# A memory set between gathers, gates turned at two places, and reciprocals spread later, in a two-layer mixture-of-experts kernel

## The chip, the cores and the metric

One core of a Trainium2 chip. The metric is the device time of one execution in microseconds, as the median of several runs. Times inside an execution come from a profiled execution, counted from the start of its span.

## What is computed

Two transformer layers over x of 8 batches x 256 tokens x 128 channels, all in float32. Each layer is modulated: six rows per batch (`sa, ca, ga, sb, cb, gb`) are made from a small matrix product.

```python
h = layernorm(x) * (1 + ca) + sa
x = x + ga * attention(h)                # causal, 16 heads
h = layernorm(x) * (1 + cb) + sb
x = x + gb * ffn(h)
```

Layer 0's heads have 8 channels, layer 1's 64. Layer 0's ffn is a shared expert (128 to 512 to 128, gelu) plus 8 routed experts of the same shape, of which each token takes the best two by softmax, weighted by their normalised shares. Layer 1's ffn returns `h + shared(h) + sum of two of 16 experts`, each `silu(h wg) * (h wu) @ wd` with 64 hidden channels, chosen by sigmoid scores.

## The kernel before

The kernel is written in a tile framework on bass. The order of instructions on every engine is the order of the program text; the framework inserts the waits between engines from the reads and writes of tiles. A tile with a tag takes one of the tag's `bufs` buffers and waits for the last readers of what was in it. A general path at the end runs only if a number called `bad` says so.

Tokens are in 16 tiles of 128, four to a group `w` (0 to 3), two to a batch `b`. Layer 0's attention is a loop of 24 units (three a batch), layer 1's of 32 (four a batch). Work that is not attention (norms, routing, moving tokens) is hung on units through three tables: `at(n, ...)` runs early in unit n, `at_end(n, ...)` at its end, in the order of registration, `at_head(n, head, ...)` behind the mask of a head.

**Routing.** A token is sent to its experts by an indirect DMA that GpSimd issues (a scatter, L932), into a DRAM table `xs` sorted by expert. Tiles of 128 rows of `xs` then go through their expert, results are written to the DRAM table `ys` (by SP), and indirect DMAs bring them back by token (a gather, L1058). `Sorted.gather(yg, j)` issues two for token tile j. In layer 0, each scatter follows a memory set of one column on GpSimd, `apart_on_gpsimd` (L1404): `nc.gpsimd.memset(most, P - 0.5)`. The tile `most` (L1076) is also a constant of the program: `flag` (L2023) compares a count of good softmax sums with it to make `bad`. `flag` comes in two steps: a reduction on VectorE (`whole`, L2026), then a matmul `good_cnt` and, on VectorE, the comparison L2030:

```python
cnt = pp.tile([1, 1], F32, tag="s", name="good_cnt")
nc.tensor.matmul(out=cnt, lhsT=whole, rhs=nums[:, 1:2], start=True, stop=True)
nc.vector.tensor_scalar(bad, cnt, most[0:1, :], 1.0, ALU.is_lt, ALU.mult)
```

**Layer 0's gates.** After routing, each token's weights stand in `gates`; `turn_gates0(w)` (L1283) transposes four tiles' gates on PE into a PSUM tile `gp` of the tag "p" (two buffers, shared with norms, logits, ranks, and projections) and copies them to SBUF as `gT`, which later multiplies the experts' output biases (L1306). `first_gates` makes the first eight tiles' gates at the end of units 17 and 20. For w = 0 and 1 the turning stands at the end of unit 23, the last; for w = 2 and 3 it stands inside the loop over layer 0's expert tiles.

**Layer 1's end.** After the last attention unit, the last batch's softmax sums are inverted (`reciprocals1`, L1708). `spread_last(us)` (L1727) spreads them over partitions: for each of two head groups u, two matmuls `rp` (L1733) into a PSUM tile of the tag "s" (two buffers), and a product into `ou` on VectorE (L1737); `finish1` (L1739) reads it. Interleaved with it, groups of four expert tiles pass through `turn1(m)` (transposes `xT` on PE, a copy on ScalarE, the next row load on SP), `hidden1(m)` (matmuls `gu` into tag "s", Silu on ScalarE, product `aq` on VectorE) and `project_tiles(m)` (matmuls `yq` into one buffer each of the tags "o" and "sum", two copies on VectorE, the write to `ys`). `norms[0]` and `norms[1]` are the norms of the last two batches in steps, `go6` and `go7` their routing steps, `tables` VectorE work that makes the tables of rows.

Then come, in the text: `gather1(j)` for the twelve token tiles of groups 0 to 2 (24 gathers); `gate_rows` and shared-expert work; `flag`'s first step; and group 3, which goes through all its experts densely. `dense_hidden(p)` is four matmuls `gud` into a buffer of tag "s", a Silu on ScalarE (L1936) and a product on VectorE (L1937), which frees the buffer. `flag`'s second step stands between `dense_hidden(2)` and `dense_hidden(3)`. `dense_gate`, `dense_project`, `combine1` (matmuls that add the gathered rows, L2018), and `ffn1_add` follow to the end.

Of the kernel before, what the change touches and what calls it, by code (L numbers as in the profile page):

```python
# [557 lines left out]
def fast_path(ctx: ExitStack, tc: tile.TileContext, i: dict, out: bass.AP, bad: bass.AP):  # L558
# [3 lines left out]
    nc = tc.nc  # L562
# [15 lines left out]
    def ps_ln(shape, name):  # L578
        return pp.tile(shape, F32, tag="p", name=name)
# [281 lines left out]
    class Sorted:  # L861
# [190 lines left out]
                in_offset=bass.IndirectOffsetOnAxis(ap=self.widx[:, d : d + 1], axis=0),  # L1052
            )

        def gather(self, yg, j):

            for k in range(2):
                nc.gpsimd.indirect_dma_start(  # L1058
                    out=yg[:, k, :], out_offset=None, in_=self.ys[:, :],
                    in_offset=bass.IndirectOffsetOnAxis(ap=self.yidx[:, j, k : k + 1], axis=0),  # L1060
                )
# [13 lines left out]
    SPANS0 = ((0, 2), (2, 2), (4, 1), (5, 1), (6, 1), (7, 1))  # L1075
# [126 lines left out]
    def norm0(bs):  # L1202

        kept = []
        name = f"0b{bs[0]}"

        def tokens():
            b, half = bs[0] // 2 * 2, bs[0] % 2
            if not half:
                tokens0["all", b] = ap0.tile([P, 4, P], F32, tag="ht", bufs=2, name=f"ht{name}")  # L1210
            ht = tokens0[bs] = tokens0["all", b][:, bass.ds(2 * half, 2 * bs[1]), :]
            if bs[1] == 1:
                tp = ps_ln([P, 2, P], f"tp{name}")
                for j in range(2):
                    nc.tensor.transpose(tp[:, j, :], h[b // 2][:, bass.ts(2 * half + j, P)], ident)
                nc.scalar.copy(ht, tp)
                return
            nc.gpsimd.tensor_tensor(by_batch(ht), by_batch(kept[0]), rows_of_span(mdb0[:, CB - 1], bs), ALU.mult)
            nc.gpsimd.tensor_tensor(by_batch(ht), by_batch(ht), rows_of_span(mdb0[:, SB - 1], bs), ALU.add)

        first = 2 * (bs[0] % 2)
        return [
            *layernorm_parts(
                bs[0] // 2, md[0], SB, CB, name, ps_ln, lambda w, xn: kept.append(xn),
                range(first, first + 2 * bs[1]),
            ),
            tokens,
        ]
# [54 lines left out]
    def turn_gates0(w):  # L1283
        gp = ps_ln([P, P], f"gp0_{w}")
        nc.tensor.transpose(gp, gates[:, bass.ts(w, TT), :].rearrange("p j e -> p (j e)"), ident)
        gT = hid0["g", w] = ap0.tile([P, P], F32, tag="gT", bufs=2, name=f"gT0_{w}")
        if w < 2:
            nc.scalar.copy(gT, gp)
        else:
            nc.vector.tensor_copy(gT, gp)  # L1290

    def shared_project0(w):
        for _ in shared_project_steps0(w):
# [100 lines left out]
    def at_end(n, *steps):  # L1394
        ends.setdefault(n, []).extend(steps)
# [28 lines left out]
    for w in range(1, NW):  # L1424
        measure, normalise, modulate = layernorm_parts(w, md[0], SA, CA, f"0a{w}", ps_ln)
        n = 6 * w - 6
# [6 lines left out]
    ways = {}  # L1433
# [9 lines left out]
    for bs in SPANS0[:4]:  # L1443
        n = 3 * sum(bs) + 2
# [18 lines left out]
    at_end(17, first_gates)  # L1463
    at_end(20, first_gates)
    norm6, norm7 = norm0(SPANS0[4]), norm0(SPANS0[5])
    at_end(23, norm6[0], lambda: turn_gates0(0), lambda: turn_gates0(1), lambda: ways[SPANS0[3]]())

    project0(0)
    project_v0(0)
# [7 lines left out]
    z1 = Sorted(xp, "1", E1, 3 * TT, ND1)  # L1477
# [93 lines left out]
    for _ in range(4):  # L1571
        hides[2]()
    one(shared_add0(1))()
    turn0(0)
    later = {
        1: tables, 2: tables, 3: tables, 5: lambda: turn_gates0(2), 7: lambda: turn_gates0(3),
        6: lambda: judge(rs0.rearrange("p b s k m -> p (b s k m)")),
    }
# [148 lines left out]
    def spread_last(us):  # L1727

        aT = st1["ou", B - 1]
        for u in us:  # L1730
            rp = pp.tile([P, 2, S], F32, tag="s", name=f"rp1_{u}")
            for m in range(2):
                nc.tensor.matmul(  # L1733
                    out=rp[:, m, :], lhsT=sel[:, u, m].rearrange("p n d -> p (n d)"), rhs=st1["r", B - 1],
                    start=True, stop=True,
                )
            nc.vector.tensor_tensor(aT[:, :, u, :], aT[:, :, u, :], rp, ALU.mult)  # L1737
# [118 lines left out]
    def weights1(m, t):  # L1856

        rows = bass.ts(t % 2, I1)
        if m < E1 // 4:
            e = 4 * m + t  # L1860
            return w1["wg1"][:, bass.ts(e, I1)], w1["wu1"][:, bass.ts(e, I1)], w1["wd1"][rows, e // 2, :]
        wt = sq["w", m]
        return wt[:, t, 0:I1], wt[:, t, I1 : 2 * I1], wt[rows, t, 2 * I1 :]

    def turn1(m):
        xT_ps = ps_ln([P, 4, P], f"xT1_{m}")
        xg = sq.pop(("x", m))
        for t in range(4):
            nc.tensor.transpose(xT_ps[:, t, :], xg[:, t, :], ident)
        xT = sq["xT", m] = lp.tile([P, 4, P], F32, tag="xT", name=f"xTs1_{m}")  # L1870
        nc.scalar.copy(xT, xT_ps)
        if m + 4 < NQ:
            fetch_rows1(m + 4)

    def hidden1(m):
        xT = sq.pop(("xT", m))
        gu = pp.tile([P, 2, 2, P], F32, tag="s", name=f"gu1_{m}")
        for what in range(2):
            for t in range(4):
                nc.tensor.matmul(  # L1880
                    out=gu[bass.ts(t % 2, I1), what, t // 2, :], lhsT=weights1(m, t)[what],
                    rhs=xT[:, t, :], start=True, stop=True,
                )
        a = sq["a", m] = lp.tile([P, 2, P], F32, tag="aq", name=f"aq1_{m}")
        nc.scalar.activation(a, gu[:, 0], AF.Silu)
        nc.vector.tensor_tensor(a, a, gu[:, 1], ALU.mult)

    def project_tiles(m):
        a = sq.pop(("a", m))
        y = [pp.tile([P, 2, P], F32, tag=tag, bufs=1, name=f"yq1_{m}_{tag}") for tag in ("o", "sum")]  # L1890
        for t in range(4):
            k = t % 2
            nc.tensor.matmul(
                out=y[k][:, t // 2, :], lhsT=a[bass.ts(k, I1), t // 2, :], rhs=weights1(m, t)[2],
                start=True, stop=True,
            )
        ysb = lp.tile([P, 2, 2, P], F32, tag="ysb", bufs=3, name=f"ysb1_{m}")
        for k in range(2):
            nc.vector.tensor_copy(ysb[:, :, k, :], y[k])
        nc.sync.dma_start(  # L1900
            out=z1.ys[bass.ds(4 * m * P, 4 * P), :].rearrange("(t p) c -> p t c", p=P),
            in_=ysb.rearrange("p a k c -> p (a k) c"),
        )
# [93 lines left out]
    sums, diags = {}, {}  # L1997

    def gather1(j):
        k, n = divmod(j, 3)  # L2000
        if n == 0:
            sums["yg", k] = lp.tile([P, 3, 2, P], F32, tag="pt", bufs=4, name=f"yg1_{k}")
        z1.gather(sums["yg", k][:, n], j)

    def weigh1(w):

# [36 lines left out]
    for j in range(2):  # L2043
        gather(1, j)
# [8 lines left out]
    for j in range(2):  # L2053
        at_head(0, 1 + 2 * j, lambda j=j: gather(2, j))
        at_head(1, 1 + 2 * j, lambda j=j: gather(3, j))
    at_end(1, lambda: combine(2))
    at_end(2, lambda: combine(3))
    for w in range(1, NW):
        n = 8 * w
# [10 lines left out]
    for b in range(B - 1):  # L2070
        n = 4 * b + 6 if b < B - 2 else N - 1
        at(n, *[lambda b=b, u=u: normalise1(b, u) for u in range(4)])
        at_end(n, lambda b=b: finish1(b))
    for bs in ((0, 2), (2, 2), (4, 1), (5, 1)):
        n = 4 * sum(bs) + 2
# [66 lines left out]
    norms[0][0]()  # L2142
    project_tiles(2)
    hidden1(4)
    spread_last((0, 1))
    turn1(5)
    norms[0][1]()
    project_tiles(3)
    norms[0][2]()
    spread_last((2, 3))  # L2150
    turn1(6)
    project_tiles(4)
    hidden1(5)
    go6()
    finish1(B - 1)
# [25 lines left out]
    for j in range(TT * LAST):  # L2181
        gather1(j)
# [54 lines left out]
def adaln_two_layers(tc: tile.TileContext, i: dict, out: bass.AP):  # L2237
    nc = tc.nc
    with tc.tile_pool(name="flag", bufs=1) as fp:
        bad = fp.tile([1, 1], mybir.dt.int32, name="bad")  # L2240
        fast_path(tc, i, out, bad)
        redo = nc.values_load(bad[0:1, 0:1], min_val=0, max_val=1, skip_runtime_bounds_check_because="a comparison")
        with tc.If(redo > 0):
            general_path(tc, i, out)
# [84 lines left out]
```

## Time and profile before

| | |
|---|---|
| median of 3 runs | 571.47 us (570.83 to 574.68) |
| profiled execution | 605.66 us, its span 603.8 us |
| mean granted TensorE clock in it | 0.963 |
| busy in the span | PE 541.5 us (90%), DVE 322.0 (53%), POOL 271.1 (45%), ACT 263.4 (44%) |

Engines are PE (TensorE), DVE (VectorE), ACT (ScalarE), POOL (GpSimd) and SP (which issues the ordinary DMAs). The page gives the span in 40 equal slices of 15.1 us, with the busy share of each engine in tenths. A line of the timeline has start, duration, engine, line of the kernel, operation, output and inputs, shapes, and in brackets the idle time before it and what ended it. A line of the waits has who waited, for what, and the sum, the number and the longest of the waits in us. PE's ends are modelled; an idle engine that nothing waits for costs nothing.

### The profile page before, as it was taken

What the parts mean: (1) busy time and instruction counts of PE and PEld (TensorE: products, weight loads), DVE (VectorE), ACT (ScalarE), POOL (GpSimd) and SP (SyncE); (2) the same over time, 40 slices, a digit from 0 to 9 for tenths busy, and PEclk for the clock granted to TensorE, in tenths of its full rate; (3) what the DMA queues carried; (4) which work ended last, traced back from release to release, by engine and by line L of the source; (5) the groups of instructions that cost most, each with busy time, mean ns of one, the idle gap of its engine ahead of it and who ended that gap; (6) DMA issues with size and microseconds to landing.
All of it is one profiled execution on the core that took longest, in us unless ns stands there. A gap on an engine that the chain in (4) does not pass through costs nothing.

```text
span 603.8 us, 11998 instructions
## 1 busy us (share of the span) xinstructions
PE 541.5 (90%) x4499; PEld 384.0 (64%) x4499; DVE 322.0 (53%) x986; ACT 263.4 (44%) x494; POOL 271.1 (45%) x400
## 2 busy tenths in 40 slices
PE   5999988899999998999999999999989988980594
PEld 4355544467999996666766676767657666840164
DVE  5258784675422224564466657556483867660153
ACT  3678765344566632664344433462535332250110
POOL 5224575665444213756222645331563540687300
PEclk9999997899999999999999999999999999986698
DMA  8699994134999812203030221203030365662311
GB/s 279 242 400 406 393 358 181 62 104 129 313 338 350 288 34 100 94 23 89 10 72 7 53 54 48 56 3 71 18 89 10 86 181 166 174 144 55 82 39 56
DMA packets 53566, 85.40 MB, mean 141 GB/s; under 512 B 6652, under 2 KB 32764, under 8 KB 52348
## 3 DMA queue, kind: packets, MB, share of 16 engines
q1 hardware_dynamic: 45308, 60.50, 31.6%
q0 software_dynamic: 8048, 23.67, 12.3%
q8 instruction: 37, 0.61, 0.4%
q10 hardware_dynamic: 144, 0.39, 0.2%
q14 instruction: 29, 0.24, 0.1%
HBM read 53.46 MB, written 31.07 MB: 140 GB/s over the span
## 4 chain that ended last, share of the span: by engine, by line
PE 72%; DVE 13%; issue 6%; DMA 3%; ACT 3%; SPq 1%; POOL 1%; another core or an unknown queue 0%; DVEq 0%; POOLq 0%; ACTq 0%
PE sc L1670 6%; PE hp L1353 6%; PE yt L1361 6%; PE o L1692 6%; PE qp L1639 5%; PE sc L1120 5%; PE y L1745 4%; PE kp L1639 4%; PE vp L1652 4%; PE o L1154 3%; PE sum L1700 3%; PE gud L1942 3%; PE hp L1273 2%; PE qk L1084 2%; PE ysh L1302 1%
## 5 line engine op out<-in xcount | busy, mean ns | idle before, releaser
L822 POOL TENSOR_SCALAR_AFFINE_SELECT pt<-pt 128x256 f32<-128x256 f32 (+1 forms) x144 | 68.0, 499 | 154.6 <-ACT pt L1673 115.3
L1058 POOL DMA_INDIRECT yg<-ys,yidx x56 | 54.4, 971 | 38.8 <-DMA ys<-ysb 20.4
L1673 ACT ACTIVATE pt<-sc 128x768 f32<-128x768 f32 x64 | 48.4, 808 | 26.2 <-PE sc L1670 26.1
L1136 ACT ACTIVATE pt<-sc 128x1024 f32<-128x1024 f32 x48 | 46.6, 1027 | 21.6 <-PE sc L1120 15.8
L1670 PEld LDWEIGHTS sc<-q,k 64*128 64x128 f32 x512 | 41.5, 187 | 18.9 <-issue 13.9
L1670 PE MATMUL sc<-q,k 64*128 64x256 f32 (+1 forms) x512 | 50.5, 336 | 0.0
L1692 PE MATMUL o<-pt,v 128*64 128x256 f32 (+1 forms) x512 | 49.0, 332 | 1.7 <-DVE ou L1704 1.7
L1355 ACT ACTIVATE hst<-hp,wt 128x128 f32<-128x128 f32 x136 | 38.9, 369 | 25.7 <-ACT hst L1355 24.6
L1655 ACT COPY v<-vp 128x512 f32<-128x512 f32 x32 | 18.8, 587 | 67.1 <-PE vp L1652 67.1
L1050 POOL DMA_INDIRECT wt<-in_wpk_dram,widx x31 | 29.6, 953 | 33.8 <-PE xT L1344 28.8
L1692 PEld LDWEIGHTS o<-pt,v 128*64 128x64 f32 x512 | 32.0, 136 | 18.9 <-POOL pt L822 5.7
L1643 DVE COPY q<-qp 128x512 f32<-128x512 f32 x32 | 22.0, 689 | 36.4 <-PE qp L1639 36.4
L1120 PE MATMUL sc<-qm,k 32*128 32x512 f32 x192 | 36.0, 726 | 3.8 <-ACT pt L1136 3.2
L1639 PE MATMUL qp<-h,wq 128*128 128x256 f32 x128 | 36.0, 404 | 3.3 <-DVE q L1643 2.0
L1366 DVE COPY ysb<-yt 128x128 f32<-128x128 f32 x39 | 11.4, 292 | 50.0 <-PE yt L1361 50.0
L932 POOL DMA_INDIRECT xs<-ht0b,idx x32 | 32.1, 1003 | 12.0 <-issue 11.4
L1652 PE MATMUL vp<-wv,h 128*128 128x512 f32 x64 | 36.0, 645 | 0.0
L1353 PE MATMUL hp<-xTs,wt 128*128 128x128 f32 x272 | 35.9, 275 | 0.0
L1361 PE MATMUL yt<-wt,hst 128*128 128x128 f32 x272 | 35.8, 275 | 0.0
L1353 PEld LDWEIGHTS hp<-xTs,wt 128*128 128x128 f32 x272 | 33.0, 192 | 0.0
L1361 PEld LDWEIGHTS yt<-wt,hst 128*128 128x128 f32 x272 | 33.0, 192 | 0.0
L1639 PE MATMUL kp<-h,wk 128*128 128x256 f32 x128 | 32.9, 380 | 0.0
(306 smaller groups left out, 1075.1 us busy)
## 6 DMA issues: line engine op xcount, KB each, us to landing
xs<-zero SPq DMA_DIRECT2D x1, 12288.0 KB
xs<-zero SPq DMA_DIRECT2D x1, 8192.0 KB
rb<-rd SPq DMA_DIRECT2D x14, 512.0 KB
mdb<-mrd SPq DMA_DIRECT2D x2, 2048.0 KB
xg<-xs SPq DMA_DIRECT2D x63, 64.0 KB
wt<-in_wpk_dram SPq DMA_DIRECT2D x24, 128.0 KB
wst<-in_wpk_dram SPq DMA_DIRECT2D x5, 514.0 KB
ys<-ysb SPq DMA_DIRECT2D x10, 256.0 KB
```

The source lines that it names most:

```text
L822: nc.gpsimd.affine_select(out=pt, in_=pt, compare_op=ALU.is_ge, fill=0.0, base=0, pattern=[[0, pt.shape[1]], [1, P]], channel_multiplier=-1,)
L1058: nc.gpsimd.indirect_dma_start(out=yg[:, k, :], out_offset=None, in_=self.ys[:, :], in_offset=bass.IndirectOffsetOnAxis(ap=self.yidx[:, j, ...
L1120: nc.tensor.matmul(out=sc[:, n, :].rearrange("p (a q) -> p a q", q=rhs.shape[2]), lhsT=k[r, cols], rhs=rhs, start=True, stop=u < 2,)
L1136: nc.scalar.activation(pt[:, bass.ts(half, 2), :], sc, AF.Exp)
L1353: nc.tensor.matmul(out=hp[:, c, :], lhsT=wt[:, bass.ts(c, P)], rhs=xT, start=True, stop=True)
L1355: nc.scalar.activation(hs[:, c, :], hp[:, c, :], AF.Gelu_apprx_tanh, bias=wt[:, WB + c : WB + c + 1])
L1361: nc.tensor.matmul(out=y, lhsT=hs[:, c, :], rhs=wt[:, bass.ds(WF + c * P, P)], start=(c == 0), stop=(c == FC - 1))
L1639: nc.tensor.matmul(out=ps_[:, n, :], lhsT=w1[f"w{what}1"][:, bass.ts(2 * u + n, P)], rhs=hb, start=True, stop=True)
L1652: nc.tensor.matmul(out=vp, lhsT=hb[:, bass.ts(j, P)], rhs=w1["wv1"][:, bass.ts(half, 512)], start=True, stop=True)
L1670: nc.tensor.matmul(out=sc[:, n, cols], lhsT=k[r, m, bass.ts(kb, P)], rhs=q[r, m, qs], start=True, stop=True)
L1673: nc.scalar.activation(pt, sc[:, :, 0:384], AF.Exp, scale=1.0 / math.sqrt(D1))
L1692: nc.tensor.matmul(out=o[bass.ts(n, D1), m, qs], lhsT=v[:, kb, bass.ts(4 * (u % 2) + 2 * m + n, D1)], rhs=pts[m][:, n, cols], start=(kb == ...
```

## The change

Three edits. `gather` gets a step that is run ahead of each of its DMAs; layer 1's `gather1` passes `apart_on_gpsimd`, so that each of the 24 gathers at the end has a memory set of `most` ahead of it (layer 0's gathers pass nothing). The gates of groups 0 and 1 are turned at the end of units 21 and 22 instead of both in unit 23, and all four copies of gates are VectorE's. In layer 1's end, both calls of `spread_last` stand one `project_tiles` later.

```diff
-        def gather(self, yg, j):
+        def gather(self, yg, j, between=lambda: None):
 
             for k in range(2):
+                between()
                 nc.gpsimd.indirect_dma_start(
...
         gT = hid0["g", w] = ap0.tile([P, P], F32, tag="gT", bufs=2, name=f"gT0_{w}")
-        if w < 2:
-            nc.scalar.copy(gT, gp)
-        else:
-            nc.vector.tensor_copy(gT, gp)
+        nc.vector.tensor_copy(gT, gp)
...
-    at_end(23, norm6[0], lambda: turn_gates0(0), lambda: turn_gates0(1), lambda: ways[SPANS0[3]]())
+    at_end(21, lambda: turn_gates0(0))
+    at_end(22, lambda: turn_gates0(1))
+    at_end(23, norm6[0], lambda: ways[SPANS0[3]]())
...
-        z1.gather(sums["yg", k][:, n], j)
+        z1.gather(sums["yg", k][:, n], j, apart_on_gpsimd)
...
     hidden1(4)
-    spread_last((0, 1))
     turn1(5)
     norms[0][1]()
     project_tiles(3)
+    spread_last((0, 1))
     norms[0][2]()
-    spread_last((2, 3))
     turn1(6)
     project_tiles(4)
+    spread_last((2, 3))
     hidden1(5)
```

## The prediction

> **What bounds the kernel now.** I read the page first: the span, and the rows of busy tenths in slices of 15.1 us.
>
> ```profile
> span 603.8 us, 11998 instructions
> ...
> PE   5999988899999998999999999999989988980594
> ...
> POOL 5224575665444213756222645331563540687300
> PEclk9999997899999999999999999999999999986698
> ```
>
> PE is at 8 or 9 tenths nearly everywhere, so the kernel is bound by PE in program order, with one hole: the slice 543 to 558 us, in which PE does nothing while POOL is at 8 ("0" above "8"). Layer 1's 24 gathers stand there. The waits between 530 and 600 us say who stood still:
>
> ```profile
> PEld gud L1942 <- issue: 28.0, 20, 20.1
> ACT a L1936 <- remote: 21.6, 1, 21.6
> ...
> DVE a L1937 <- issue: 20.2, 1, 20.2
> ```
>
> ScalarE waited 21.6 us ahead of one Silu whose input PE had finished, and the releaser is "remote", that is unknown. VectorE and PE only waited for ScalarE. The timeline of the same stretch:
>
> ```profile
> 530.68 5.43 POOL L1800 TENSOR_TENSOR p<-one_by_e,p 128x32 f32<-128x32 f32 x1 [0.56 <-DVE p L1796]
> ...
> 536.39 1.05 POOL L1058 DMA_INDIRECT yg<-ys,yidx  x1 [0.29 <-issue]
> ...
> 542.40 1.02 PE L1942 MATMUL gud<-h,wu 128*128 128x512 f32 x2
> ...
> 562.10 0.60 ACT L1936 ACTIVATE a<-gud 128x512 f32<-128x512 f32 x1 [21.62 <-remote]
> 562.73 0.69 DVE L1937 TENSOR_TENSOR a<-a,gud 128x512 f32<-128x512 f32 x1 [20.24 <-issue]
> ...
> 563.47 2.07 PE L1942 MATMUL gud<-h,wg 128*128 128x512 f32 x2 [19.84 <-issue]
> ...
> 565.29 0.94 POOL L1058 DMA_INDIRECT yg<-ys,yidx  x1 [0.30 <-issue]
> ```
>
> The gathers run from 536.39 to 566.23, one each 1.25 us (0.95 + 0.30 gap). Last I asked for the tile that the new memory set writes, `most`:
>
> ```profile
> L1405 POOL MEMSET most<- x32: 89/113/163, 69.0 to 139.6; 128x1 f32 x32
> L2030 DVE TENSOR_SCALAR bad<-good_cnt,most x1: 198/198/198, 572.4 to 572.4; 1x1 int32<-1x1 f32 x1
> ```
>
> It is read once, by `flag` on VectorE, in the middle of this tail. Its last write was at 139.6 us, so this read never waited. The change puts 24 new writes ahead of it.
>
> **Is the hole in the timed runs?** The profiled execution took 605.66 us (span 603.8 and 1.86 around it), the median of the runs shown is 571.47: 34.2 less. PE is idle for 603.8 - 541.5 = 62.3 us; 22.6 of them lie in 540 to 580, 8.0 in the first 20 us and some 8.5 after the last matmul. A run with the hole could save 34.2 us only out of the remaining 23 us of small waits, and would have to win 11 us more from matmuls that run back to back. Without the hole most of it is explained at once. I take it that the timed runs do not have it (9 in 10), or have a short one.
>
> **The skill.** "Runtime: NRT & Kernel Launch", the section on the preamble and postamble, gives a gap of some 6.2 us between a profile's total and the time the runtime reports; 34.2 is far more, which fits a hole of the profiled execution alone. "TensorE: Matmul & The Clock Gate", Part 1, says that after an idle window of about 3.4 us PE runs at half clock until it has been busy as long. The trace agrees in kind: the granted clock was 0.62 on average over the hole, and from the restart at 563.5 it was 0.50 up to 567.3 and 0.56 to 569.1, 5.6 us. "GPSIMD Engine Reference", section 2.1, says that what waits on a Pool instruction is released at that instruction's own completion; so a reader of `most` need not wait for the gather behind the last memory set, but for all 23 gathers ahead of it, which are in front on the same queue. "Perfetto Trace Analysis", section DMA Instruction - SWDGE (GPSIMD), says that the profiled end of a gather is the end of descriptor writing, not of the data; the 0.95 us are thus what POOL itself is held for. No run here shows more.
>
> **Part 1, the memory set.** Each costs POOL 0.113 us (row L1405). In the scatters of layer 0, which have it already, a set starts at 113.38 and the next at 114.63, the scatters between at 113.68 and 114.95: 0.96 + 0.12 + 0.19 = 1.27 us for one. For a gather of 0.95 that is 1.26 against 1.25 now: the set fills the gap. 24 x 0.01 = 0.2 us on POOL, hidden as long as the last gather is early enough (below).
>
> The wait it adds. `flag`'s second step (L2030) reads `most`, hence waits for the 24th set. POOL leaves the power at L1800 at 536.11; the first gather starts at some 536.45, the 24th at 536.45 + 23 x 1.26 = 565.43, and its set ends at 565.24. L2030 runs at 565.3 to 565.5.
>
> When would VectorE get there? Durations: a dense hidden pair 4 x 0.43 = 1.72 us on PE; from its end to the freed PSUM buffer 1.42 us (577.77 to 579.14 in the timeline, Silu 0.60 and product 0.69 in it, and 0.05 to PE). Without the hole: gud 0 ends at 543.42, its product at 544.8, the second gate copy at 545.2; gud 1 544.85 to 546.6; gud 2 to 548.3; good_cnt to 548.5; the product of gud 2 to 549.65; L2030 to 549.85; gud 3 549.7 to 551.4 in the buffer of gud 2; gud 4 from 551.4 in the buffer that good_cnt leaves. There are two such buffers (tag "s"). With the wait, VectorE stands at L2030 until 565.3. Behind it on VectorE are the product of gud 3, all dense gates and ffn1_add; good_cnt's buffer is freed by L2030, gud 3's by the product behind it, so PE stops after gud 3, and ScalarE has nothing to do. gud 4 starts at 565.55 and not 551.4: 14.15 us. PE is then cold: gud 4 takes 3.4 instead of 1.72, and about 2 us of gud 5 go at half speed (0.8 to 1.0): 2.5 us. After that the order of work is the same as before. Sum +16.65 us, nothing beside it.
>
> What is late otherwise: without the hole the last combine would start at 594.26 - 24.5 = 569.8 and its gather lands about 1 us after 566.2, so the gathers had 2.5 us to spare; there is nothing that the new wait replaces.
>
> **Part 2, the gates.** Now at the end of unit 23: gp 0 on PE, copy 0.27 (L1288), gp 1, copy; PE stands 2.06 us ahead of gp 1, again with a "remote" wait of 1.89 on ScalarE. Moved, gp 0 falls in behind unit 21's rank products at 107.6, into a free buffer, and VectorE, idle there (108.8 to 109.4), copies in 0.28 (L1290). gp 1 comes at 111.1 after tp0b and needs one of the two "p" buffers: tp0b's, freed by ScalarE's copy at 111.58, a wait of 0.6 us ahead of unit 23's scores; or the logits', freed only at 114.10, a wait of 3.0. I take the first, which comes free 2.5 us earlier. The later ranks then come at 118.5 and not at 119.9: -1.4 in the profiled execution. In a run without the 1.9 us stall it is nearly 0. With the other buffer it is +1.1 or up to +2.7. Value -0.5; bounds -1.4 and +2.7.
>
> **Part 3, the reciprocals.** PE waits 2.5 us at L1733 now, for VectorE's aq products, which stand behind the tables (502.4 to 506.3). Moved back, turn1(5) (0.66 us) fills part of that, but project_tiles(3) is then next and needs the yq buffers, freed by the copies ending at 508.14. From there project 0.55, two pairs of rp 1.8, nt1b 0.45, turn 0.6, project 0.55, two more rp 1.8: hidden1(5) at about 514.0, in the trace 514.02. spread_last issues no DMA, so SP's order and row loads stay. Value 0, bounds -0.7 and +0.7.
>
> **Sum.** 16.65 - 0.5 + 0 = +16.1 over a run without the hole. On the median: 571.47 + 16.1 = 587.6. In profiled executions the comparison can look the other way round: 603.8 - 24.5 without the hole is 579.3, and + 16.1 is 595, less than the 603.8 that contain it.
>
> **Rivals.**
> - A, the stall is real in the timed runs and the sets end it. For: it stands exactly beside the unbroken gathers. Against: the 34.2 us, and layer 0's scatters have "remote" waits (4.4 and 1.9 us) in spite of their sets. Then gud 4 moves from 575.90 to 565.55 and pays the cold clock, -10.35 + 2.5 = -7.9: 563.5. It decides if the timed runs lose over 16 us there. Chance 0.07, faster.
> - B, the stall is in the timed runs and stays, or something else already holds VectorE until 565. The new wait is covered: 571. Chance 0.07, same.
> - C, slower by less: POOL is quicker in the timed runs, or a hole of up to 6 us is there already. If a gather takes 1.0 us, the 24th set is at 559.5 and the wait 8.4: +10, 581.5. Inside the forecast's range.
> - The change does what it says in that the gathers are kept apart; that it helps is what A says.
>
> **Numbers.** Forecast 587.6, chance 0.86 for slower. 1% (5.7 us) is about what a measurement of this kernel can tell from no change. Range 577 to 592: below, C with the lower bound of part 2 and a wait of some 7; above, part 2 at +2.7 and a PE that stays cold for longer. A and B are left out.
>
> **What would show it.** In the profile after: L2030 directly behind the 24th set at about 565, its releaser POOL `most`; PE idle between gud 3 and gud 4; no gap of 20 us ahead of gud 1; 24 sets between 536 and 566 with 1.26 us spacing; gp at 107 and 111, gT on VectorE. Wrong if L2030 doesn't wait for POOL, if it starts before 558, or if gud 4 starts long before it.

## The result, and the profile after

The changed kernel takes 588.43 us (median; 588.18 to 592.09) where the kernel before takes 571.41 (570.83 to 574.68): a ratio of 1.030, 95% interval 1.025 to 1.035, or 17.0 us more. The forecast was 587.6 us, slower. Its main step, a new wait of VectorE, stands in the profile as described. Its statement on the 20 us hole in the profile of before needs a correction, which the second half of the experiments gives. Times below are medians of all executions of a kernel; a ratio leaves out executions more than 1.5% above the fastest of their kernel and can differ by some 0.002 from the quotient of two medians.

The profiled execution took 588.29 us, 586.6 of it span, and so stands for the timed runs. From its page, the span and the same three rows (slices of 14.7 us now):

```profile
span 586.6 us, 12022 instructions
...
PE   5999989899999998999999999999999998987094
...
POOL 5224577773544123656221635532373460478800
PEclk9999999999999999999999999999999999899697
```

There is again one slice in which PE is nearly off ("0") while POOL is at 8. It looks like the hole of before, but the reason is another one. The view of the tile `most` (duration least/median/most in ns, then first and last start) and the waits between 520 and 586 us (total us, times, longest) tell it:

```profile
L1403 POOL MEMSET most<- x56: 88/118/125, 67.9 to 556.4; 128x1 f32 x56
L2030 DVE TENSOR_SCALAR bad<-good_cnt,most x1: 205/205/205, 556.5 to 556.5; 1x1 int32<-1x1 f32 x1
its engine sat idle before it (us, times) until:
  POOL most L1403: 15.6, 1
```

```profile
ACT a L1936 <- PE gud L1942: 33.4, 8, 16.7
DVE bad L2030 <- POOL most L1403: 15.6, 1, 15.6
...
PE gud L1942 <- DVE bad L2030: 13.8, 1, 13.8
```

No wait is "remote" any more. VectorE stands 15.6 us at L2030, a 1x1 operation of 0.2 us, until POOL's last set; PE stands 13.8 us for VectorE; ScalarE stands for PE. The timeline of the place:

```profile
540.96 1.12 PE L1942 MATMUL gud<-h,wg 128*128 128x512 f32 x2 [1.29 <-DVE a L1937]
...
556.38 0.12 POOL L1403 MEMSET most<- 128x1 f32 x1
556.53 0.20 DVE L2030 TENSOR_SCALAR bad<-good_cnt,most 1x1 int32<-1x1 f32 x1 [15.63 <-POOL most L1403]
556.69 0.95 POOL L1059 DMA_INDIRECT yg<-ys,yidx  x1 [0.19 <-issue]
556.79 2.07 PE L1942 MATMUL gud<-h,wg 128*128 128x512 f32 x2 [13.85 <-DVE bad L2030]
...
560.05 1.02 PE L1942 MATMUL gud<-h,wg 128*128 128x512 f32 x2
```

The lines of PE are the first halves of gud 3, gud 4 and gud 5. The set at 556.38 is the 24th, with 23 gathers ahead of it on POOL, and L2030 starts as soon as it is done; the last gather is not waited for. The lines below show PE's clock coming back after the pause (stretch, its length, busy time of PE, PEld, DVE, ACT and POOL, then the granted clock as a share of full speed, and two figures on DMA):

```profile
559.00:560.00 1.00, 1.00 (x2) 0.30 (x1) 0.00 (x0) 0.00 (x0) 0.00 (x0) 0.64 0.00 0
560.00:562.00 2.00, 2.00 (x8) 0.99 (x7) 1.12 (x2) 0.63 (x2) 0.00 (x0) 1.00 0.01 4
```

### The profile page after: what moved, and what is told of

Same layout as the page of the kernel before. It is cut to its first block, busy times and chain, and to the rows that moved or that the text cites. A ratio compares the mean times of both kernels' runs of the same rounds, so it can differ in the third digit from the quotient of the medians.

```text
span 586.6 us, 12022 instructions
## 1 busy us (share of the span) xinstructions
PE 533.4 (91%) x4499; PEld 381.3 (65%) x4499; DVE 324.5 (55%) x988; ACT 263.2 (45%) x492; POOL 272.0 (46%) x424
## 4 chain that ended last, share of the span: by engine, by line
PE 57%; DVE 8%; POOL 6%; issue 3%; DMA 3%; ACT 2%; SPq 0%; POOLq 0%; ACTq 0%; DVEq 0%
PE sc L1670 7%; PE hp L1351 6%; PE yt L1359 6%; PE o L1692 6%; PE qp L1639 5%; PE vp L1652 5%; PE kp L1639 5%; PE y L1745 4%; POOL yg L1059 4%; PE sum L1700 3%; PE gud L1942 1%; DMA ys<-ysb 1%; PE of L1952 1%; PE hp L1274 1%; PE ysh L1300 1%
## 5 line engine op out<-in xcount | busy, mean ns | idle before, releaser
L1121 PE MATMUL sc<-qm,k 32*128 32x512 f32 x192 | 33.6, 675 | 1.9 <-ACT pt L1137 1.3
L1643 ACT COPY k<-kp 128x512 f32<-128x512 f32 x32 | 18.8, 588 | 32.4 <-PE kp L1639 32.4
```

Of the source, the lines that this page charges most:

```text
L1643: copy(st1[what, b, u], ps_)
```

## The experiments

Theory W: the whole loss is VectorE's new wait at L2030 for the last set. Rivals: S, the sets themselves slow POOL or what runs beside it; G, the moved gates and reciprocals carry a good part. The first four kernels ran on one chip, where the kernel before took 573.5 us.

### As many sets, but where nobody reads them

```diff
-    most = xp.tile([P, 1], F32, name="most")
+    most = xp.tile([P, 2], F32, name="most")
 ...
-        nc.gpsimd.memset(most, P - 0.5)
+        nc.gpsimd.memset(most[:, 0:1], P - 0.5)
 ...
-        z1.gather(sums["yg", k][:, n], j, apart_on_gpsimd)
+        z1.gather(sums["yg", k][:, n], j, lambda: nc.gpsimd.memset(most[:, 1:2], P - 0.5))
 ...
-        nc.vector.tensor_scalar(bad, cnt, most[0:1, :], 1.0, ALU.is_lt, ALU.mult)
+        nc.vector.tensor_scalar(bad, cnt, most[0:1, 0:1], 1.0, ALU.is_lt, ALU.mult)
```

> The changed kernel, but `most` has two columns: the 24 sets between the gathers go to column 1, and `flag` reads column 0, whose last write lies in layer 0. As many sets at the same places, no wait for them. Theory W (the whole loss is the new wait of VectorE for the 24th set): the loss is gone, 571 us (569.5 to 572.5); `bad` at L2030 starts about 541 us with no POOL wait, gud 4 about 543. Rival S (the sets themselves slow POOL, the gathers or VectorE, by stretching what runs beside them): it stays at 580 or more. Rival G (parts 2 and 3 carry a good part): it stays above 574.

572.55 us, ratio 0.999 (0.997 to 1.001): the loss is gone with all 24 sets in place. Its timeline:

```profile
537.75 0.20 DVE L2030 TENSOR_SCALAR bad<-good_cnt,most 1x1 int32<-1x1 f32 x1
...
539.71 1.02 PE L1942 MATMUL gud<-h,wg 128*128 128x512 f32 x2
...
541.42 1.02 PE L1942 MATMUL gud<-h,wg 128*128 128x512 f32 x2
...
553.69 0.11 POOL L2003 MEMSET most<- 128x1 f32 x1
553.99 0.94 POOL L1059 DMA_INDIRECT yg<-ys,yidx  x1 [0.19 <-issue]
```

L2030 carries no bracket: it waits for nothing, 16 us ahead of the last set. gud 4 (539.71) and gud 5 (541.42) follow at once. The time stands at the edge of what was expected; the kernel before itself took 573.5 us on this chip and not 571.4. On this chip S is out.

### The sets alone

The kernel before with the first part of the change only: `between` in `gather`, and `apart_on_gpsimd` handed to it in `gather1`.

```diff
-        z1.gather(sums["yg", k][:, n], j)
+        z1.gather(sums["yg", k][:, n], j, apart_on_gpsimd)
```

> The kernel before with the sets alone; gates and reciprocals as before. W: all of the loss is here, 588.5 us (587 to 590), L2030 waits some 15 us for POOL. G: clearly less than 588, for instance 580, the rest being due to the moved gates and reciprocals.

588.32 us, ratio 1.026 (1.021 to 1.031). That is 14.8 us over the kernel before on this chip. The wait at L2031 (here one line further down) is 15.2 us. All of the loss that can be told apart is in this part.

### Gates and reciprocals alone

```diff
-        z1.gather(sums["yg", k][:, n], j, apart_on_gpsimd)
+        z1.gather(sums["yg", k][:, n], j)
```

> The changed kernel without the sets: the moved gates and reciprocals alone. W: 571 us (569.5 to 573), gud 4 follows gud 3 at once. G: above 574. Is the 20 us hole of the profiled run of the kernel before a property of gathers without sets? If it is, it shows in this profile too, whose own execution is then about 590 to 605 us; if it was an accident of one execution, this profiled execution is within 1% of the timed ones and has no `remote` wait above 5 us.

573.63 us, ratio 1.002 (1.000 to 1.005): at most some 2.6 us over the kernel before. It lies just above the 573 that W allowed and below the 574 of G, both of which were set for a kernel before of 571.4 us and not 573.5. G is out as a main cause. The profile has no "remote" wait, and its own execution took 571.60 us. So gathers without sets do not as such produce the hole that the profile of before shows.

### One set in place of 24

```diff
             for k in range(2):
-                between()
+                if 2 * j + k == 23:
+                    between()
```

> The changed kernel with a single set in place of 24, ahead of the last gather. W: the cost follows the place of the last set, not their number: 588 us (587 to 590), the same as with 24. S: the cost follows the number, 1/24 of 17 us, so 572 us.

588.71 us, ratio 1.026 (1.023 to 1.029). From its view of `most`:

```profile
L1404 POOL MEMSET most<- x33: 88/117/124, 68.7 to 557.2; 128x1 f32 x33
L2031 DVE TENSOR_SCALAR bad<-good_cnt,most x1: 205/205/205, 557.3 to 557.3; 1x1 int32<-1x1 f32 x1
its engine sat idle before it (us, times) until:
  POOL most L1404: 15.6, 1
```

A single set of 0.1 us costs as much as 24. What is paid for is its place: behind 23 gathers. This is also what "GPSIMD Engine Reference", section 2.1, in the Trainium skill leads to: the waiting instruction is released at the set's own completion, however little the set does.

### The parts that were forecast near nothing, each alone

These two and the next two ran on a second chip, and the kernel before took 604.4 us there. It is a footing of its own: comparisons are made within it.

```diff
-    at_end(23, norm6[0], lambda: turn_gates0(0), lambda: turn_gates0(1), lambda: ways[SPANS0[3]]())
+    at_end(21, lambda: turn_gates0(0))
+    at_end(22, lambda: turn_gates0(1))
+    at_end(23, norm6[0], lambda: ways[SPANS0[3]]())
```

with VectorE's copy for every `w` in `turn_gates0`:

> The kernel before with the moved gates (part 2) alone. Forecast -0.5 us with bounds -1.4 and +2.7 against the kernel before; a ratio below 0.9975 or above 1.0047 would put it outside. Its profile should show gp0 and gp1 ahead of the place where they stood, with VectorE's copies.

605.21 us, ratio 1.002 (1.000 to 1.005), by the ratio +1.5 us with the interval from -0.2 to +3.1. The lines for the two products:

```profile
107.76 0.45 PE L1285 MATMUL gp<-ident,gates 128*128 128x128 f32 x1
...
111.97 0.33 PE L1285 MATMUL gp<-ident,gates 128*128 128x128 f32 x1 [0.46 <-ACT ht0b L1216]
...
119.59 0.17 PE L917 MATMUL rk<-marks,before 128*128 128x16 bf16 x1 [0.46 <-DVE marks L909]
```

Both products stand where the forecast put them, the second after a wait of 0.46 us for ScalarE's copy. But the ranks start at 119.59, against 119.90 before.

The reciprocals:

```diff
     hidden1(4)
-    spread_last((0, 1))
     turn1(5)
 ...
     project_tiles(3)
+    spread_last((0, 1))
     norms[0][2]()
-    spread_last((2, 3))
     turn1(6)
     project_tiles(4)
+    spread_last((2, 3))
```

> The kernel before with the reciprocals spread one group of tiles later (part 3) alone. Forecast 0, bounds -0.7 and +0.7 us against the kernel before (ratio 0.999 to 1.001). PE's wait of 2.5 us ahead of the aq products moves to the next project_tiles and does not go.

604.29 us, ratio 1.000 (0.996 to 1.004). The interval is too wide to test 0.7 us; the profiles show the step itself. Waits of PE between 485 and 520 us, first in the kernel before, then in this kernel:

```profile
PE rp L1733 <- DVE aq L1886: 2.5, 2, 1.8
```

```profile
PE yq_o L1893 <- DVE ysb L1899: 2.4, 1, 2.4
```

The wait moves from the spread to the next project_tiles and stays about as long.

### `flag` behind the gathers: with the sets and without

```diff
-    next(judged)
     shared_project(2)
 ...
-    next(judged, None)
     dense_hidden(3)
 ...
     ffn1_add(1)
+    next(judged)
+    next(judged, None)
```

With the 24 sets of the changed kernel:

> The changed kernel with all 24 sets, but both steps of `flag` (the reduction, the product good_cnt, and `bad`) stand behind ffn1_add(1) instead of in the middle of the dense pairs. W: VectorE comes to `bad` when the 24th set is done or nearly done, and nothing that PE needs is queued behind it, so the loss of 17 us goes, and with it the 1.29 us that PE waits ahead of gud 3 for the buffer that good_cnt takes: 0 to -1.5 us against the kernel before (ratio 0.997 to 1.000). Rival (only the address shared with the sets matters, as a delay on POOL): still 580 or more.

And in the kernel before, without sets:

> The kernel before (no sets) with `flag` behind ffn1_add(1). Only the buffer wait of 1.29 us ahead of gud 3 can go: 0 to -1.3 us against the kernel before. If the timed runs of the kernel before had the 20 us hole ahead of gud 1, moving a later instruction would not touch it. Its profile is one more look for the hole: W expects none (the profiled execution within 1% of the timed ones).

With sets 610.84 us, ratio 1.010 (1.004 to 1.016); without 602.93, ratio 0.998 (0.996 to 1.001). Theory W, which promised no loss with sets, fails on this chip: VectorE no longer waits for POOL, and 6 us are lost all the same. First with sets, then without: the last gather, the dense Silus that waited for a late signal of PE, and gud 1 where PE starts again.

```profile
562.48 0.94 POOL L1059 DMA_INDIRECT yg<-ys,yidx  x1 [0.19 <-issue]
...
567.77 0.60 ACT L1936 ACTIVATE a<-gud 128x512 f32<-128x512 f32 x1 [31.27 <-remote]
...
569.14 2.07 PE L1942 MATMUL gud<-h,wg 128*128 128x512 f32 x2 [28.25 <-DVE a L1937]
```

```profile
562.21 0.60 ACT L1936 ACTIVATE a<-gud 128x512 f32<-128x512 f32 x1 [21.67 <-remote]
...
563.59 2.08 PE L1942 MATMUL gud<-h,wg 128*128 128x512 f32 x2 [19.84 <-DVE a L1937]
...
565.34 0.94 POOL L1058 DMA_INDIRECT yg<-ys,yidx  x1 [0.30 <-issue]
...
570.65 0.60 ACT L1936 ACTIVATE a<-gud 128x512 f32<-128x512 f32 x1 [7.84 <-remote]
```

Here is the hole of the profile of before (there 21.62 us, "remote", PE 19.84), in a kernel whose timed runs take 603 us. It is no accident of one execution: it goes with a chip on which this kernel takes 30 us longer. (Each chip was used at one time only, so chip and time can't be told apart.) All four kernels of this chip show it, with 16 to 31 us ahead of a dense Silu; none of the four of the first chip does, nor does the profile after.

And the sets do not end it. With them no signal gets through until 4.4 us after the last gather's issue is over (563.42 to 567.77). Without them the signal of gud 0 comes 4 us before that point, PE starts gud 1 inside the burst, and the next one that is held, that of gud 1, comes 4.4 us after it (566.28 to 570.65). From the start of gud 0 to that of gud 4 it is 37.4 us with the sets (538.69 to 576.12) and 32.4 without (541.55 to 573.96): 5.0 us more. Against the kernel before the median is up by 6.4. Whether moving `flag` takes the loss away where there is no hole was not tested: both runs of this edit with sets met the hole.

### The changed kernel, and 18 sets, once more

The last four ran together on a third chip, where the kernel before takes 600.8 us. The hole is in all four of their profiles (22.8 to 29.8 us ahead of a dense Silu). The changed kernel as it is:

> The changed kernel as it is, to see on which footing it stands where the kernel before takes 570 and where it takes 604 us (four runs so far saw a kernel before of 573.5 us, four others one of 604.4 us, with a `remote` wait of 16 to 31 us ahead of a dense Silu). W: where the kernel before has no such hole, ratio 1.026 to 1.030. Where it has the hole (before near 604), the wait for POOL ends about where the hole ends, so the loss is mostly covered: ratio 0.99 to 1.015. Theory A in its form for such a chip (the sets end the hole): 586 to 590 against 604, ratio 0.97 to 0.98.

With sets ahead of the first 18 gathers only:

```diff
-                between()
+                if 2 * j + k < 18:
+                    between()
```

> The changed kernel with sets ahead of the first 18 of the 24 gathers only. W: the wait ends with the 18th set, 6 x 1.25 = 7.5 us earlier than with 24; gud 4 is late by 6.1 to 6.4 us instead of 13.85, the cold clock costs 1.5 again, so the loss is 7.6 to 9 us of 17 (ratio 1.013 to 1.016 where the kernel before has no hole). If the loss followed the number of sets it would be 18/24 of 17 = 12.7 us (ratio 1.022).

And the two kernels with the late `flag`, with sets and without:

> The changed kernel with 24 sets and `flag` behind ffn1_add(1), once more. W: where the kernel before has no hole, the loss is gone and the 1.29 us wait ahead of gud 3 too: ratio 0.997 to 1.000. Where it has one, as in the first run of this edit: 1.005 to 1.015, with a `remote` wait of some 30 us ahead of gud 0's Silu.

> The kernel before with `flag` behind ffn1_add(1), no sets, once more. Where the kernel before has no hole: ratio 0.997 to 1.000, since only the wait of 1.29 us for good_cnt's buffer can go. Where it has one: 0.998, as in the first run of this edit.

| kernel | us | ratio to before (95%) |
|---|---|---|
| changed kernel | 607.84 | 1.011 (1.005 to 1.017) |
| 18 sets | 607.43 | 1.011 (1.006 to 1.015) |
| late flag, 24 sets | 606.65 | 1.011 (1.008 to 1.013) |
| late flag, no sets | 603.53 | 1.003 (1.000 to 1.005) |

From the changed kernel's profile on this chip:

```profile
568.00 0.94 POOL L1059 DMA_INDIRECT yg<-ys,yidx  x1 [0.19 <-issue]
...
573.09 0.60 ACT L1936 ACTIVATE a<-gud 128x512 f32<-128x512 f32 x1 [29.58 <-remote]
...
574.46 2.07 PE L1942 MATMUL gud<-h,wg 128*128 128x512 f32 x2 [28.09 <-DVE a L1937]
...
581.80 0.20 DVE L2030 TENSOR_SCALAR bad<-good_cnt,most 1x1 int32<-1x1 f32 x1
```

L2030 has no bracket: the sets were over at 568, and VectorE came 14 us later. The wait that costs some 15 us on the first chip, and 17.0 in the result, is wholly covered by the hole. Moving `flag` away therefore saves nothing here (1.011 both times). What the profile shows in its place is the longer hole: again 4.2 us beyond the last gather's issue (568.94 to 573.09). That this is the whole of the loss is not shown. The kernel with 18 sets was to show the loss following the place of the last set; under the hole it could not, so that remains shown only by the single set. Its profile, of its fastest execution, has a hole like that without sets (PE 19.8 us, and 32.8 us from gud 0 to gud 4), yet its median is no better than with 24; what it loses is not settled. The late `flag` without sets, expected at 0.998, gains nothing either.

## Why the prediction was right, point by point

- **The wait at L2030.** VectorE was to stand from 549.65, the end of gud 2's product, to 565.3, which is 15.65 us, directly behind the 24th set: 15.63 measured, and 0.03 us between the set's end and L2030. The spacing of 1.26 us was 1.26 on average (first gather at 527.65, the 24th at 556.69).
- **The sign of being wrong that came up.** L2030 started at 556.53, ahead of the 558 that was named. The limit was a time of the profile of before. There the gathers begin at 536.39, 8.74 us later than in the profile after, and the forecast 565.3 less 8.74 is 556.56. The limit was misplaced, and the wait was not.
- **gud 4 late by 14.15 us.** From the start of gud 3 to that of gud 4 it is 15.83 us after, and 1.82 in the kernel with the sets in the other column: 14.01.
- **The cold clock, 2.5 us: the term that was mis-sized.** gud 4 took 3.26 us in place of 1.71, which is 1.55; gud 5, which was to pay 0.8 to 1.0, ran at full speed. The forecast used the 5.6 us of slow clock read after the hole of before. Here the granted clock was 0.50 up to 559, and 0.64 from 559 to 560, so full speed came some 2.9 us after the restart, nearer to the 3.4 us of "TensorE: Matmul & The Clock Gate", Part 1, in the Trainium skill. One measured value could not be carried over, as the last section shows.
- **Nothing else moves.** From gud 5 to PE's last combine it is 16.76 us after, and 16.77 with the other column. The sum of the part is thus 14.01 + 1.55 = 15.6, where 16.65 was forecast; the medians on the first chip give 14.8 for the sets alone and 15.2 for the single set over the kernel before, and 15.8 and 16.2 over the other column.
- **Gates, -0.5.** The buffer chosen (tp0b's) and its wait (0.6 forecast, 0.46 measured) were right. The gain was not: the ranks came 0.3 us earlier, not 1.4. Three runs bear on it, by their ratios: +1.5 alone, +1.2 with the reciprocals, and -0.6 (-1.9 to +0.7) in the kernel with the sets in the other column, which has both as well. All lie within the bounds of -1.4 and +2.7, and none is told apart from nothing, so the value of this part stays open.
- **Reciprocals, 0.** The wait went to project_tiles as described: 2.5 us before, 2.4 with the reciprocals alone. The time of this part is not resolved.
- **The total.** That 588.4 came within 1 us of 587.6 is in part luck. The terms that can be read add up to 15.6, one us under the forecast for them; the 17.0 measured has an interval of 14.3 to 19.8, and the rest is not assigned.
- **The hole.** That the timed runs do not have it was right for the runs shown, and the budget of 34.2 us that led to it was sound. "The profiled execution alone" was wrong: on two other chips it is in every profile that was taken, and the kernel before takes 601 to 604 us in its timed runs, as in the profile of before (605.66). The profile of before has the marks of such a chip, and most likely it was taken on one; the runs do not say so themselves. The 595 us for a profile after followed from the same mistake: it took the hole out of a profile of such a chip and left the other time in that the profile after does not have, 8.7 us of it ahead of the gathers. The profiled execution of the changed kernel took 588.3 without the hole and 613.0 with it.
- **The rivals.** A fails on both footings: where the hole exists the sets lengthen it. B describes the chips with the hole rightly in its wait, which is covered, but not in its time, which is 1% longer. C is out: the gathers keep their spacing, and no shorter hole stands in the profiles of the first chip.

No version beats the kernel before. Sets that nobody reads (0.999, without the hole), and the late flag without sets (0.998 and 1.003, with it), equal it.

## What to carry to other kernels

An instruction that only fills or separates must write where nobody reads: a reader of its output waits for all that is queued ahead of it on its engine, and everything queued behind the reader waits too. When a profiled execution's own time is far from the median, take the profile for another footing, and compare kernels only within one. A cure for a stall is to be judged where the stall occurs, and its price where it does not.

## What the runs showed of the hardware

- On two of the three chips of the experiments PE's signal of a finished product came 13 to 27 us late beside the burst of 24 gathers. In the profile of before, the matmuls of gud 0 are recorded up to 543.42 us, and the update of PE's semaphore stands at 562.08; without the hole (the kernel without sets) it is 535.01 and 535.02. This is what the waits call "remote": an update with no instruction ending beside it. Smaller ones of 1.9 to 5.2 us stand beside layer 0's scatters in six of the nine profiles with the hole, in spite of the sets between the scatters.
- In all nine of these profiles the last held Silu starts 3.6 to 4.4 us after the end of the last gather's issue, with the sets or without. With 24 sets no signal of a dense product came before that point (4.2 to 4.4 us after it, three profiles). Without sets, and with 18, the first one came 1.4 to 9.8 us ahead of that end. Why some chips hold the signals back, and why the sets matter, stays open: no experiment touched it.
- In the clock records of all fourteen profiles, every change of the granted clock lies a whole number of steps of 3.41 us from the one before: at 546.07, 559.73 and 580.21 us in the profile after (4 and 6 steps apart), at 548.40, 568.88, 572.29 and 575.70 in that of before (6, 1 and 1). What a restart pays therefore depends on where it falls between two steps: full speed came 2.9 us after the restart in the profile after (556.79 to 559.73), 3.5 with the sets and the late `flag` on the second chip (569.14 to 572.66), and 5.4 in the profile of before (563.47 to 568.88).
